# Attention A: one mask matmul goes behind the scores, and TensorE's other work is dealt out anew over the phases

## The chip, the core and the metric

The kernel runs on one core of a Trainium2 chip. The core has five engines that work side by side, each with its own queue of instructions: TensorE (PE in the profile; its weight loads are PEld), VectorE (DVE), ScalarE (ACT), GpSimd (POOL) and SyncE (SP, which here only issues DMAs). TensorE writes to PSUM, eight banks of 128 partitions x 512 F32 values; VectorE and ScalarE read PSUM; GpSimd works on SBUF. The metric is device time in microseconds from the first to the last instruction and what little lies around it; lower is better.

## The reference

The program is a stack of four layers over x of 2 x 1024 x 512 (F32): attention A, a small mixture of experts, attention B, the same mixture again. Each adds its result to x. The change touches attention A alone, cut here to what matters:

```python
q = (query @ Wq).reshape(bsz, tgt_len, 2 * H, D)      # H = 16 heads in pairs, D = 16
k = (query @ Wk).reshape(bsz, tgt_len, 2 * H, D)
v = (query @ Wv).reshape(bsz, tgt_len, H, 2, D)
...                                                    # rotary embedding on q and k
attn1 = causal_attn_pair(q1, k1, v1, v2, mask, scale)  # softmax(q1 k1) v, causal, 1024 x 1024
attn2 = causal_attn_pair(q2, k2, v1, v2, mask, scale)
...
f1 = jnp.fft.rfft(attn1, axis=1)
f2 = jnp.fft.rfft(attn2, axis=1)
attn_freq = f1 - lambda_full * f2                      # then a fixed low-pass filter along time
attn = jnp.fft.irfft(attn_freq * filt, n=tgt_len, axis=1)
...                                                    # RMS norm per head, then @ Wout
```

Query is the layer-normed x. Each of the 16 heads has two score matrices (q1 k1 and q2 k2); since the filter is linear, the kernel subtracts the second softmax, times lambda, from the first before it multiplies by the values, and applies the filter as a small set of matmuls.

## The kernel before, in words

**Units and phases.** Attention A is cut into 16 units (`NU`), each one batch and two heads. A unit has nine phases (`NP`); its rows of 128 queries are j = 0 to 7 for two heads h, and row j needs 128 x (j+1) columns of keys. `PHASES` pairs rows so that each phase has 1024 columns: phases 0 and 1 hold rows 7 of both heads, phases 2 to 7 a row 6, 5 or 4 and a row 0, 1 or 2 of the other head, phase 8 both rows 3. Step t of the main loop issues the scores of phase t (`now`), joins the softmaxes of phase t-1 (`last`) and transposes the weights of phase t-2 (`old`). So "step 7" of a unit is the turn of the loop in which the scores of its phase 7 are issued; it joins phase 6 and transposes phase 5.

**One step on each engine.** The order is written by hand (`tc.manual_schedule`) for TensorE, VectorE, ScalarE and GpSimd; the DMA issues on SP are placed by the framework. The functions named are in the listing below.

- TensorE: `scores` (two mask matmuls per PSUM bank that holds a diagonal block, L475, then the score matmuls, L488; `mm` is 0 for the first score matrix and 1 for the second), four transposes (first half of `transpose`, L578), the step's "large" pieces, four more transposes.
- VectorE: `minima` of the first score matrix (L502 or L510; the scores are held negated, so the least is the softmax's maximum), the reciprocal of `divide` (L545), `minima` of the second, `join` (L554), and what `finish` (L633, L634) has to do.
- ScalarE: the copy of the first four transposes (L580), `exponentials` (L519), the copy of the other four, the copies of the large pieces out of PSUM.
- GpSimd: `share` (L539) and the product in `divide` (L547), which make the factor `ratio` of `join`; then the step's "middle" work, above all `rotate` (three tensor operations, L399 to L401, for half of the time of one unit's q and k); then the "rear" work, above all `fold` (L651 to L654, eight small sums and differences of one unit's result).

**Large pieces.** The tables fill the dictionary `large`, step by step: `project` (four per unit: q and k of the next unit, 256 columns of time each, steps in `PROJECT`), `project_values` (one or two 128-column value tiles, steps in `VALUES`), `weigh` (weights times values; `PARTS` cuts it in two: rows 7, 6, 0 at step 6, the other rows at step 2 of the next unit), `finish` (transposes the sum back and divides it; steps 7, and 4 of the next unit) and, in the first units, `spread_half` (transposes of the second batch's x; `SPREAD`). All pieces of a step share one PSUM bank (`misc`), which comes free when their results have been read. Behind the second and the fourth projection of a unit ScalarE copies the result to `raw`, two DMAs make `other`, and `rotate` runs two steps after the projection (`at(middle, ... + 2, rotate, ...)`), followed by the DMAs to `keys` and, for one half, `swapped`. `fold` of unit n runs in step 6 of unit n+1, behind the step's middle work.

**Scores' buffers.** The score tiles have three buffers of two banks each (`ps_s`); the second score matrix of a phase takes the buffer of the first one of the phase before, so its first matmul waits for that one's exponentials.

Of the kernel before, what the change touches and what calls it, by code (L numbers as in the profile page):

```python
# [2 lines left out]

# [1 line left out]

# [6 lines left out]
F32 = mybir.dt.float32  # L12
# [13 lines left out]
NQ = 4  # L26
# [52 lines left out]
def hybrid_layer_kernel(ctx: ExitStack, tc: tile.TileContext, i: dict, out: bass.AP):  # L79
# [67 lines left out]
    with ExitStack() as sa:  # L147
# [8 lines left out]
        with ExitStack() as sp:  # L156
# [277 lines left out]
            def scores(n, ph):  # L434
                rows = PHASES[ph]
                if ph == 0:
                    least[n] = tally.tile([P, 16, 2], F32, tag="least", name=f"least_{n}")
                    sums[n] = [
                        tally.tile([P, 16], F32, tag=f"sums{mm}", name=f"sums{mm}_{n}") for mm in range(2)
                    ]  # L440
                key = f"{n}_{ph}"
                s = [ps_s.tile([P, T], F32, tag="s", name=f"s{mm}_{key}") for mm in range(2)]
                ps = [
                    work.tile([P, T], F32, tag=f"p{mm}", name=f"p{mm}_{key}", bufs=(4, 2)[mm])
                    for mm in range(2)
                ]
# [24 lines left out]
                opened = {d0 // 512 for d0 in masks}  # L471
                width = P * len(masks) // len(opened)
                for d0 in masks[0 : len(opened)]:
                    for mm in range(2):
                        nc.tensor.matmul(  # L475
                            s[mm][:, d0 : d0 + width],
                            eye[:, 0, :],
                            eye[:, 1 : 1 + width // P, :].rearrange("p k q -> p (k q)"),
                            start=True,
                            stop=False,  # L480
                        )
                ends = {c0 // 512: c0 for _, _, c0, _, _ in pieces}
                for h, j, c0, s0, w in pieces:
                    group, back = (1 - h, T // 2) if s0 >= 512 else (h, 0)
                    q, k = (swapped[n][:, 0, :], swapped[n][:, 1, :]) if s0 >= 512 else (qk[n], keys[n % 2])
                    for mm in range(2):
                        r0 = 64 * group + 32 * mm
                        nc.tensor.matmul(  # L488
                            s[mm][:, c0 : c0 + w],
                            q[r0 : r0 + 32, j * P - back : (j + 1) * P - back],  # L490
                            k[r0 : r0 + 32, s0 - back : s0 - back + w],
                            start=(c0 // 512 not in opened),
                            stop=(ends[c0 // 512] == c0),
                        )
                held[n, ph] = s, ps, spans

            def minima(n, ph, mm):
# [66 lines left out]
            def transpose(n, ph, half):  # L564
# [11 lines left out]
                for k in range(4):  # L576
# [4 lines left out]

            PARTS = [
                (0, 3, [[(0, 7, 0)], [(1, 7, 0)], [(0, 6, 0), (0, 0, P)], [(1, 6, 0), (1, 0, P)]]),
                (
                    3,
                    8,
                    [
                        [(0, 5, 0), (0, 3, P)],  # L590
                        [(1, 5, 0), (1, 3, P)],
                        [(0, 4, 0), (0, 2, P), (0, 1, 2 * P)],
                        [(1, 4, 0), (1, 2, P), (1, 1, 2 * P)],
                    ],
                ),
            ]

            def weigh(bank, c0, n, part):
                _, _, groups = PARTS[part]
                po = bank[:, c0 : c0 + P * (part + 2)]  # L600
# [12 lines left out]
                yield  # L613

                full = P * (part + 1)
                oT = work.tile([P, 3 * P], F32, tag="oT", name=f"oT_{n}_{part}")
                nc.scalar.copy(oT[:, 0:full], po[:, 0:full])
                nc.scalar.copy(oT[64:P, full : full + P], po[64:P, full : full + P])
                turned[n, part] = oT

            def finish(bank, c0, n, part):
                oT = turned[n, part]
                lo, hi, _ = PARTS[part]
# [10 lines left out]
                nc.vector.tensor_mul(  # L634
                    results[n][:, lo:hi, :].rearrange("p r (h f) -> p r h f", h=2),
                    tp.rearrange("p (r h f) -> p r h f", h=2, f=32),
                    rec[:, :, :, None].to_broadcast([P, hi - lo, 2, 32]),
                )
# [47 lines left out]

            SPREAD = [n * NP + k for n in range(6) for k in (1, 5, 8)][1:]
            for j in range(JT):
                t = SPREAD[2 * j]
                at(rear, t - 4, load_x, JT + j)  # L690
# [3 lines left out]
                for half in range(2):  # L694
                    at(large, SPREAD[2 * j + half], spread_half, 256, j, half)
            for half in range(2):
                at(rear, (2 * NQ - 2) * NP + PROJECT[3 - 2 * half], bring, half)
# [776 lines left out]
```

## Time and profile before

| | |
|---|---|
| three runs, median (lowest to highest) | 1141.25 us (1139.06 to 1142.85) |
| the profiled execution, span | 1142.6 us |
| attention A, first to last phase's scores | 35.0 to about 700 us |
| units 10 to 13, first mask to first mask | 40.28 us each |
| units 1 to 6 | 43.24, 41.01, 43.58, 41.00, 41.48, 43.46 us |
| units 7 to 9 | 39.95, 42.05, 41.57 us |
| busy in unit 12: PE, DVE, ACT, POOL | 38.8, 36.5, 36.5, 19.5 us |

The unit lengths are the distances between the first mask matmuls (L475) of consecutive units in the trace. Busy time is a sum over a stretch; it says how much work an engine had, not when it had to wait. In a timeline line, the first number is the start from the span's beginning, the second the duration of the merged instructions, and the bracket gives the idle time of the engine ahead of them and the instruction that ended it. Lines merged as "x4" are four instructions.

### The profile page before, as it was taken

How to read it: one execution, taken by the hardware profiler on the slowest of the kernel's cores; microseconds unless marked ns; L12 is line 12 of the kernel's file. 1: busy time of each engine (PE TensorE's matmuls, PEld its weight loads, DVE VectorE, ACT ScalarE, POOL GpSimd, SP SyncE). 2: the span in 40 equal slices, each digit the busy share in tenths (PEclk: the TensorE clock that was granted, in tenths of full speed). 3: DMA queues.
4: the chain of work that ended last, by engine and by line, in shares of the span. 5: the costliest groups of instructions: out<-in, count | busy, mean ns of one | idle time of the engine just before them, and what ended most of it. 6: DMA issues, size and time to landing. Idle time of an engine off the chain costs nothing.

```text
span 1142.6 us, 23491 instructions
## 1 busy us (share of the span) xinstructions
PE 1067.2 (93%) x8680; PEld 732.3 (64%) x8680; DVE 930.8 (81%) x2046; ACT 766.9 (67%) x2010; POOL 438.1 (38%) x689
## 2 busy tenths in 40 slices
PE   6899999999889999999999979889999999999997
PEld 5777777777677877777777655544555455554554
DVE  5699999999889889889989998577787777758677
ACT  3588988989879889899999877243433433443433
POOL 1246446345345444534535672122323223223300
PEclk9999999999989999999999999889999999999999
DMA  5212222211301101110110521200000000001002
GB/s 176 79 42 67 80 80 66 71 38 52 116 15 39 42 16 38 48 33 25 39 43 16 182 114 39 111 1 1 0 1 1 1 1 1 1 1 37 1 19 92
DMA packets 33345, 52.19 MB, mean 46 GB/s; under 512 B 6480, under 2 KB 11088, under 8 KB 33104
## 3 DMA queue, kind: packets, MB, share of 16 engines
q1 hardware_dynamic: 33072, 50.44, 13.8%
q8 instruction: 69, 1.13, 0.4%
q14 instruction: 44, 0.36, 0.1%
q10 hardware_dynamic: 160, 0.26, 0.1%
HBM read 23.42 MB, written 6.29 MB: 26 GB/s over the span
## 4 chain that ended last, share of the span: by engine, by line
PE 55%; DVE 26%; ACT 11%; issue 5%; POOL 2%; DMA 1%; SPq 0%; DVEq 0%; POOLq 0%; ACTq 0%
DVE least L510 8%; PE s L488 8%; ACT p L519 7%; DVE p L554 6%; PE pq_q L1224 5%; PE py L1287 5%; PE bank L355 4%; PE pq_v L1224 4%; PE dtp L578 4%; PE pq_k L1224 4%; PE z L1028 3%; PE bank L605 3%; DVE least L502 3%; PE hr_f L1092 2%; PE y L978 2%
## 5 line engine op out<-in xcount | busy, mean ns | idle before, releaser
L519 ACT ACTIVATE p<-s,least 128x640 f32<-128x640 f32 (+7 forms) x512 | 378.3, 744 | 41.9 <-DVE least L510 27.9
L510 DVE TENSOR_REDUCE least<-s 128x1 f32<-128x896 f32 (+5 forms) x384 | 244.2, 679 | 35.4 <-PE s L488 35.4
L554 DVE SCALAR_TENSOR_TENSOR p<-p,ratio,p 128x1024 f32<-128x1024 f32 (+7 forms) x256 | 227.0, 922 | 3.5 <-POOL ratio L547 3.4
L578 PE MATMUL dtp<-ident,p 128*128 128x128 f32 x1152 | 184.8, 283 | 14.1 <-ACT dt L580 7.9
L580 ACT COPY dt<-dtp 128x512 f32<-128x512 f32 x288 | 168.9, 586 | 42.9 <-PE dtp L578 39.5
L488 PE MATMUL s<-keys,qk 32*128 32x128 f32 (+3 forms) x1408 | 169.0, 445 | 0.0
L578 PEld LDWEIGHTS dtp<-ident,p 128*128 128x128 f32 x1152 | 128.8, 142 | 58.2 <-ACT dt L580 30.4
L502 DVE TENSOR_REDUCE least<-s 128x1 f32<-128x1024 f32 (+1 forms) x96 | 115.9, 1213 | 26.5 <-PE s L488 26.5
L488 PEld LDWEIGHTS s<-keys,qk 32*128 32x128 f32 x1408 | 94.2, 188 | 49.3 <-issue 43.0
L547 POOL TENSOR_TENSOR ratio<-ratio,inverse 128x2 f32<-128x2 f32 (+1 forms) x144 | 28.1, 195 | 243.0 <-DVE inverse L545 217.9
L539 POOL TENSOR_TENSOR ratio<-sums,neg_lam 128x2 f32<-128x2 f32 (+1 forms) x144 | 73.6, 511 | 117.9 <-ACT p L519 117.6
L355 PE MATMUL bank<-xnT,wqk 128*128 128x256 f32 x472 | 115.8, 389 | 2.8 <-ACT raw L366 1.8
L488 PE MATMUL s<-swapped 32*128 32x128 f32 (+2 forms) x896 | 104.8, 345 | 0.0
L519 ACT ACTIVATION_READ_ACCUMULATOR p<-s,least 128x1 f32 x512 | 104.2, 203 | 0.0
L355 PEld LDWEIGHTS bank<-xnT,wqk 128*128 128x128 f32 x472 | 86.0, 192 | 18.0 <-ACT raw L366 5.6
L488 PEld LDWEIGHTS s<-swapped 32*128 32x128 f32 x896 | 71.0, 185 | 9.5
L475 PE MATMUL s<-eye 128*128 128x256 bf16 (+1 forms) x320 | 60.8, 251 | 16.5 <-ACT p L519 15.5
L605 PE MATMUL bank<-dt,v 128*32 128x128 f32 x2304 | 69.5, 274 | 1.7 <-ACT v L387 0.7
L605 PEld LDWEIGHTS bank<-dt,v 128*32 128x32 f32 x2304 | 60.9, 110 | 8.0 <-ACT v L387 4.4
L400 POOL TENSOR_TENSOR other<-other,rope_a_sb 128x512 f32<-128x512 f32 x30 | 63.0, 2099 | 0.0
L1247 POOL TENSOR_TENSOR qkv_v<-qkv_v,qkv_k 128x512 f32<-128x512 f32 x16 | 20.4, 1274 | 108.5 <-DVE qkv_v L1246 107.4
L379 PE MATMUL bank<-wval,xnT 128*128 128x128 f32 x448 | 60.4, 282 | 0.8
(222 smaller groups left out, 1790.8 us busy)
## 6 DMA issues: line engine op xcount, KB each, us to landing
other<-raw SPq DMA_DIRECT2D x64, 128.0 KB, 2.1
xin<-in_query SPq DMA_DIRECT2D x16, 256.0 KB, 2.9
keys<-qk SPq DMA_DIRECT2D x64, 64.0 KB, 1.9
swapped<-keys SPq DMA_DIRECT2D x32, 128.0 KB, 2.3
x_sb<-in_query SPq DMA_DIRECT2D x16, 256.0 KB, 6.3
out_dram<-x_sb SPq DMA_DIRECT2D x16, 256.0 KB, 2.2
swapped<-qk SPq DMA_DIRECT2D x30, 128.0 KB, 2.3
wqk<-in_w_qk SPq DMA_DIRECT2D x8, 256.0 KB, 2.8
```

The costliest lines, as they stand in the source:

```text
L355: nc.tensor.matmul(pp, wqk[:, part, c, :], xnT[b, half][:, c, t0 : t0 + 256], start=(c == 0), stop=(c == EC - 1),)
L400: engine.tensor_mul(other, other, rope_a[:, 1, cols])
L488: nc.tensor.matmul(s[mm][:, c0 : c0 + w], q[r0 : r0 + 32, j * P - back : (j + 1) * P - back], k[r0 : r0 + 32, s0 - back : s0 - back + w], ...
L502: nc.vector.tensor_reduce(least[n][:, e[0] : e[-1] + 1 : e[-1] - e[0] or 1, mm], s[mm].rearrange("p (g k) -> p g k", g=g), AX.X, ALU.min,)
L510: nc.vector.tensor_reduce(least[n][:, e, mm : mm + 1], s[mm][:, c0 : c0 + w], AX.X, ALU.min)
L519: nc.scalar.activation(ps[mm][:, c0 : c0 + w], sv, AF.Exp, bias=low, scale=-1.0, accum_out=sums[n][mm][:, e : e + 1],)
L539: nc.gpsimd.tensor_mul(ratio[:, w], first, neg_lam.to_broadcast([P, w.stop]))
L554: nc.vector.scalar_tensor_tensor(ps[0][:, c0 : c0 + w], ps[1][:, c0 : c0 + w], ratio[:, k : k + 1], ps[0][:, c0 : c0 + w], ALU.mult, ALU.add,)
L578: nc.tensor.transpose(tp[:, k * P : (k + 1) * P], d[:, c0 : c0 + P], ident)
L580: nc.scalar.copy(dt[:, 4 * half : 4 * half + 4, :], tp.rearrange("p (k q) -> p k q", k=4))
L605: nc.tensor.matmul(po[32 * g : 32 * g + 32, c0 : c0 + P], vals[n // 2 % 2][:, k, 64 * (n % 2) + 32 * h : 64 * (n % 2) + 32 * h + 32], dt[: ...
L1224: nc.tensor.matmul(pq, hTs[n][:, c, :], win(c, s), start=(c == 0), stop=(c == EC - 1))
```

## The change

In `scores`, the mask matmuls of the first score matrix stay ahead; those of the second are issued behind all score matmuls, as the last of their accumulation (the first score matmul of that bank then starts it). `weigh` is cut in three: the second sum (rows 5 to 1) becomes rows 5 and 4 at step 1 of the next unit and rows 3, 2 and 1 at step 2; its transposition (`finish`) goes from step 4 to step 5, except for the last three units. The projections of a unit go from steps 8, 0, 1, 3 to 8, 0, 3, 4, except for the last unit, and the `rotate` of the fourth goes with it from step 5 to step 6. The value tiles are at steps 2, 5, 7 (1, 1, 2 tiles) where they were at 4, 5, 7 (1, 2, 1), with fewer exceptions, and the transposes of the second batch's x at steps 1, 4, 8 where they were at 1, 5, 8; the loads, statistics and scalings of that x are counted from there. `fold` keeps its step 6.

```diff
+                def mask(mm, first):
+                    for d0 in masks[0 : len(opened)]:
                         nc.tensor.matmul(
                             s[mm][:, d0 : d0 + width],
                             eye[:, 0, :],
                             eye[:, 1 : 1 + width // P, :].rearrange("p k q -> p (k q)"),
-                            start=True,
-                            stop=False,
+                            start=first,
+                            stop=not first,
                         )
-                ends = {c0 // 512: c0 for _, _, c0, _, _ in pieces}
+                mask(0, True)
...
                 for h, j, c0, s0, w in pieces:
...
+                        if bank not in opened:
+                            start = True
+                        else:
+                            start = mm == 1 and begins[bank] == c0
...
+                            start=start,
+                            stop=ends[bank] == c0 and not (mm == 1 and bank in opened),
                         )
+                mask(1, False)
...
-            PARTS = [
-                (0, 3, [[(0, 7, 0)], [(1, 7, 0)], [(0, 6, 0), (0, 0, P)], [(1, 6, 0), (1, 0, P)]]),
...
+            PARTS = [(0, 3), (3, 8)]
+            WEIGHED = [
+                (0, 0, True, [[(0, 7, 0)], [(1, 7, 0)], [(0, 6, 0), (0, 0, P)], [(1, 6, 0), (1, 0, P)]]),
+                (1, 0, False, [[(0, 5, 0)], [(1, 5, 0)], [(0, 4, 0)], [(1, 4, 0)]]),
+                (1, P, True, [[(0, 3, 0)], [(1, 3, 0)], [(0, 2, 0), (0, 1, P)], [(1, 2, 0), (1, 1, P)]]),
             ]
...
-                for blocks in zip(*order):
-                    for g, (h, j, c0, k) in enumerate(blocks):
+                for blocks in zip_longest(*order):
+                    for g, block in enumerate(blocks):
+                        if block is None:
+                            continue
+                        h, j, c0, k = block
...
-                oT = work.tile([P, 3 * P], F32, tag="oT", name=f"oT_{n}_{part}")
-                nc.scalar.copy(oT[:, 0:full], po[:, 0:full])
-                nc.scalar.copy(oT[64:P, full : full + P], po[64:P, full : full + P])
-                turned[n, part] = oT
+                if base == 0:
+                    turned[n, part] = work.tile(
+                        [P, (part + 2) * P], F32, tag=f"oT{part}", name=f"oT_{n}_{part}", bufs=1
+                    )
+                oT = turned[n, part]
+                nc.scalar.copy(oT[:, base : base + P], po[:, 0:P])
+                if half:
+                    nc.scalar.copy(oT[64:P, base + P : base + 2 * P], po[64:P, P : 2 * P])
...
-                for part, (t_sum, t_end) in enumerate(((6, 7), (NP + 2, NP + 4 - (n >= NU - 2)))):
-                    at(large, t + t_sum, weigh, P * (part + 2), n, part)
-                    at(large, t + t_end, finish, (192, 320)[part], n, part)
+                for piece, when in enumerate((6, NP + 1, NP + 2)):
+                    at(large, t + when, weigh, (2, 1, 2)[piece] * P, n, piece)
+                for part, when in enumerate((7, NP + (5 if n < NU - 3 else 4 if n < NU - 2 else 3))):
+                    at(large, t + when, finish, (192, 320)[part], n, part)
                 at(rear, t + NP + (3 if n == NU - 1 else 6), fold, n)
...
-            PROJECT = (-1, 0, 1, 3)
-            VALUES = {p: [(k, w) for k, w in ((-14, 1), (-13, 2), (-11, 1), (-5, 1), (-4, 2), (-2, 1))] for p in range(1, 8)}
-            VALUES[4] = [(-5, 1), (-4, 2), (-2, 1), (0, 1), (4, 1), (5, 2)]
-            VALUES[5] = [(-11, 1), (-10, 1), (-9, 1), (-8, 1), (-5, 1), (-4, 2), (-2, 1)]
-
-            SPREAD = [n * NP + k for n in range(6) for k in (1, 5, 8)][1:]
+            PROJECT = [(-1, 0, 3, 4)] * (NU - 1) + [(-1, 0, 1, 3)]
+            VALUES = {p: [(-16, 1), (-13, 1), (-11, 2), (-7, 1), (-4, 1), (-2, 2)] for p in range(1, 8)}
+            VALUES[4] = [(-13, 1), (-11, 2), (-7, 1), (-7, 1), (-4, 1), (-2, 2)]
+
+            SPREAD = [n * NP + k for n in range(6) for k in (1, 4, 8)][1:]
...
-                    if t + PROJECT[piece] >= 0:
-                        at(large, t + PROJECT[piece], project, 256, u, piece)
+                    when = t + PROJECT[u][piece]
+                    if when >= 0:
+                        at(large, when, project, 256, u, piece)
                     if piece % 2:
-                        at(middle, t + PROJECT[piece] + 2, rotate, u, 1 - piece // 2)
+                        at(middle, when + 2, rotate, u, 1 - piece // 2)
```

More of the change, by code (lines that the diff above doesn't have):

```diff
@@ L2 @@
 from contextlib import ExitStack
+from itertools import zip_longest
 import numpy as np
@@ L472, in scores @@
                 width = P * len(masks) // len(opened)
-                for d0 in masks[0 : len(opened)]:
-                    for mm in range(2):
+                def mask(mm, first):
+                    for d0 in masks[0 : len(opened)]:
                         nc.tensor.matmul(
@@ L478, in scores @@
                             eye[:, 1 : 1 + width // P, :].rearrange("p k q -> p (k q)"),
-                            start=True,
-                            stop=False,
-                        )
-                ends = {c0 // 512: c0 for _, _, c0, _, _ in pieces}
+                            start=first,
+                            stop=not first,
+                        )
+                mask(0, True)
+                begins, ends = {}, {}
+                for _, _, c0, _, _ in pieces:
+                    begins.setdefault(c0 // 512, c0)
+                    ends[c0 // 512] = c0
                 for h, j, c0, s0, w in pieces:
@@ L485, in scores @@
                     q, k = (swapped[n][:, 0, :], swapped[n][:, 1, :]) if s0 >= 512 else (qk[n], keys[n % 2])
+                    bank = c0 // 512
                     for mm in range(2):
                         r0 = 64 * group + 32 * mm
+                        if bank not in opened:
+                            start = True
+                        else:
+                            start = mm == 1 and begins[bank] == c0
                         nc.tensor.matmul(
@@ L491, in scores @@
                             k[r0 : r0 + 32, s0 - back : s0 - back + w],
-                            start=(c0 // 512 not in opened),
-                            stop=(ends[c0 // 512] == c0),
+                            start=start,
+                            stop=ends[bank] == c0 and not (mm == 1 and bank in opened),
                         )
+                mask(1, False)
                 held[n, ph] = s, ps, spans
@@ L580, in transpose, with weigh @@
                 nc.scalar.copy(dt[:, 4 * half : 4 * half + 4, :], tp.rearrange("p (k q) -> p k q", k=4))
-            PARTS = [
-                (0, 3, [[(0, 7, 0)], [(1, 7, 0)], [(0, 6, 0), (0, 0, P)], [(1, 6, 0), (1, 0, P)]]),
[L586 to L595, printed above, removed]
-            ]
-            def weigh(bank, c0, n, part):
-                _, _, groups = PARTS[part]
-                po = bank[:, c0 : c0 + P * (part + 2)]
+            PARTS = [(0, 3), (3, 8)]
[3 more added lines that the diff above has]
+                (1, P, True, [[(0, 3, 0)], [(1, 3, 0)], [(0, 2, 0), (0, 1, P)], [(1, 2, 0), (1, 1, P)]]),
+            ]
+            def weigh(bank, c0, n, piece):
+                part, base, half, groups = WEIGHED[piece]
+                po = bank[:, c0 : c0 + P * (1 + half)]
                 order = [[(h, j, c0, k) for h, j, c0 in g for k in range(j + 1)] for g in groups]
-                for blocks in zip(*order):
-                    for g, (h, j, c0, k) in enumerate(blocks):
+                for blocks in zip_longest(*order):
[3 more added lines that the diff above has]
+                        h, j, c0, k = block
                         dt, at = turned[n, h, j, k]
@@ L613, in weigh @@
                 yield
-                full = P * (part + 1)
-                oT = work.tile([P, 3 * P], F32, tag="oT", name=f"oT_{n}_{part}")
-                nc.scalar.copy(oT[:, 0:full], po[:, 0:full])
-                nc.scalar.copy(oT[64:P, full : full + P], po[64:P, full : full + P])
-                turned[n, part] = oT
+                if base == 0:
[6 more added lines that the diff above has]
+                    nc.scalar.copy(oT[64:P, base + P : base + 2 * P], po[64:P, P : 2 * P])
             def finish(bank, c0, n, part):
                 oT = turned[n, part]
-                lo, hi, _ = PARTS[part]
+                lo, hi = PARTS[part]
                 tp = bank[:, c0 : c0 + 64 * (hi - lo)]
@@ L696, in hybrid_layer_kernel @@
             for half in range(2):
-                at(rear, (2 * NQ - 2) * NP + PROJECT[3 - 2 * half], bring, half)
+                at(rear, (2 * NQ - 2) * NP + PROJECT[2 * NQ - 1][3 - 2 * half], bring, half)
             for k in range(4):
```

## The prediction

> **What bounds the kernel now.** I read the page first.
>
> ```profile
> span 1142.6 us, 23491 instructions
> PE 1067.2 (93%) x8680; PEld 732.3 (64%) x8680; DVE 930.8 (81%) x2046; ACT 766.9 (67%) x2010; POOL 438.1 (38%) x689
> PE 55%; DVE 26%; ACT 11%; issue 5%; POOL 2%; DMA 1%; SPq 0%; DVEq 0%; POOLq 0%; ACTq 0%
> ```
>
> TensorE leads, VectorE stands next, POOL has more than half of its time free. Busy sums by unit of nine phases say the same of attention A (units 11 and 12):
>
> ```profile
> core 0: us, PE busy (x) PEld busy (x) DVE busy (x) ACT busy (x) POOL busy (x), PEclk, DMA share, GB/s
> 492.90:533.20 40.30, 38.93 (x452) 30.94 (x450) 36.60 (x60) 36.60 (x94) 19.49 (x32) 1.00 0.12 34
> 533.20:573.40 40.20, 38.84 (x451) 30.86 (x449) 36.51 (x60) 36.52 (x94) 19.49 (x32) 1.00 0.12 35
> ```
>
> So TensorE idles 1.4 us a unit: all that a better deal could win. But averages hide order. POOL's timeline of unit 12, phases 5 to 7 (start, duration):
>
> ```profile
> 558.49 0.20 POOL L547 TENSOR_TENSOR ratio<-ratio,inverse 128x2 f32<-128x2 f32 x1 [2.34 <-DVE inverse L545]
> 558.64 1.28 POOL L399 TENSOR_TENSOR raw<-raw,rope_a_sb 128x512 f32<-128x512 f32 x1
> 559.88 1.98 POOL L400 TENSOR_TENSOR other<-other,rope_a_sb 128x512 f32<-128x512 f32 x1
> 561.94 1.35 POOL L401 TENSOR_TENSOR qk<-raw,other 128x512 f32<-128x512 f32 x1
> 563.24 0.19 POOL L539 TENSOR_TENSOR ratio<-sums,neg_lam 128x2 f32<-128x2 f32 x1
> 563.56 0.20 POOL L547 TENSOR_TENSOR ratio<-ratio,inverse 128x2 f32<-128x2 f32 x1
> 563.71 0.46 POOL L651 TENSOR_TENSOR folded<-result 128x128 f32<-128x128 f32 x1
> ...
> 567.33 0.46 POOL L654 TENSOR_TENSOR folded<-result 128x128 f32<-128x128 f32 x1
> 567.74 0.20 POOL L539 TENSOR_TENSOR ratio<-sums,neg_lam 128x2 f32<-128x2 f32 x1
> 568.01 0.20 POOL L547 TENSOR_TENSOR ratio<-ratio,inverse 128x2 f32<-128x2 f32 x1
> ```
>
> POOL is a queue in program order. `rotate` (L399 to L401) fills the time between the ratios of steps 5 and 6, `fold` (L651 to L654) that between steps 6 and 7, with no gap in either. VectorE's `join` (L554) needs the ratio (L547):
>
> ```profile
> 559.45 2.69 DVE L554 SCALAR_TENSOR_TENSOR p<-p,ratio,p 128x768 f32<-128x768 f32 x2
> 564.52 1.46 DVE L554 SCALAR_TENSOR_TENSOR p<-p,ratio,p 128x768 f32<-128x768 f32 x2
> 568.82 1.41 DVE L554 SCALAR_TENSOR_TENSOR p<-p,ratio,p 128x640 f32<-128x640 f32 x2
> 570.43 0.36 DVE L634 TENSOR_TENSOR result<-bank,rec 128x192 f32<-128x192 f32 x1
> ```
>
> Step 7's ratio is ready at 568.21, its join starts at 568.82: 0.6 us of slack. What a late ratio does is seen once, in unit 6, where `rotate` waited 2.9 us for a DMA (DVE's, then PE's timeline, then sums by stretch):
>
> ```profile
> 318.31 1.78 DVE L554 SCALAR_TENSOR_TENSOR p<-p,ratio,p 128x768 f32<-128x768 f32 x2 [2.09 <-POOL ratio L547]
> 319.64 0.63 PE L578 MATMUL dtp<-ident,p 128*128 128x128 f32 x4 [1.63 <-DVE p L554]
> 318.00:320.00 2.00, 0.37 (x6) 0.39 (x4) 1.69 (x2) 0.69 (x4) 1.84 (x5) 1.00 0.18 66
> 322.00:324.00 2.00, 1.35 (x13) 0.99 (x15) 1.79 (x4) 2.00 (x8) 1.48 (x4) 0.50 0.00 0
> ```
>
> VectorE stood 2.09, TensorE 1.63 us, the granted clock fell to 0.5, and the unit took 43.5 us against 40.3.
>
> **TensorE's pieces, from piece to piece in unit 12.** Projection 1.73; value tile 0.99, two 1.89; old second sum 2.32 (80 instructions, ten rounds of 8); `finish` 0.57 and 0.46. The split sum needs six and five rounds: 1.39 and 1.16, so 0.23 more. Old to new: phase 1, 1.73 to 1.39; phase 2, 2.32 to 1.16+0.99=2.15; phase 4, 0.57+0.99=1.56 to 1.73; phase 5, 1.89 to 0.57+0.99=1.56; phase 7, 0.46+0.99=1.45 to 0.46+1.89=2.35; the others stay. Phases 0 to 5 lose 0.67, phase 7 gains 0.90. ACT's extra copy (0.29, phase 1) replaces one of 0.39 and hides in the ACT time that is free in each unit (3.8 us); the two `oT` tags only take waits away.
>
> **The mask.** Same matmuls and weight loads. VectorE may start one mask (about 0.11 us) sooner, and the wait for the second bank (15.5 us in 25 waits, "PE s L475 <- ACT p L519") comes one mask and one matmul pair later, some 0.3 us (phase 1's two masks and twelve score instructions take 1.29, 0.1 each). Bounds: nothing, and 25 x 0.3 = 7.5 us won; extra changes between BF16 and F32 show no gap at today's one per phase, so I allow at most 144 x 0.05 = 7 us lost. I take 2 us won, as most of these waits lie in a few units.
>
> **The step that decides.** The fourth projection moves from phase 3 to 4, and `rotate` follows two phases behind: into phase 6, where `fold` is. On POOL then stand, behind step 6's ratio: `rotate`, `fold`, and only then both instructions of step 7's ratio. Behind that ratio on VectorE: join 7, the reciprocal and product of `finish`, which frees the one bank that phase 8's projection is written to, and minima 8; on TensorE the transposes of step 8. The rotation's DMAs on SP (two for `keys`; `swapped` belongs to the other half, still in phase 2) come one phase later: about X+10 us against scores at X+16, X being the start of step 6's scores; hidden.
>
> **Smaller moves, costed at nothing.** The other half's `rotate` stays in phase 2; step 3's ratio follows it with 0.6 us to spare before its join (550.0 against 550.65), and the phase shrinks by 0.17. Three of eight `norm_scale` (POOL, 2.08 us) go from phase 4 to 3, behind that ratio; the next ratio is wanted over 4 us later. Their loads of x on SP go one phase earlier with their statistics, the distance stays. `bring` of the first half follows the projection from step 57 to 58, as does the rotation that waits for it. Pair 1's value weights are issued at the end of step 0 and now wanted in step 2 (about 5 us later; a 256 KB load lands in 2.8 us, and one of x goes ahead): 0 to 1 us lost once, taken as nothing. Pair 4's value tiles move to units 6 and 7; their x was brought in steps 54 and 58, the first tile that needs the later half comes in step 65.
>
> Round trip of a unit, old and new, in us:
> - Projection 8 to next scores (571.16 to 573.43): 2.27, 2.27.
> - Scores 0 to scores 6: 26.59; 26.59-0.67=25.92.
> - Scores 6 (559.76) to the end of step 6's ratio (563.76): 4.00. In step 5 VectorE's join falls from 2.69 to about 1.5 (step 6's, without L400 beside it, takes 1.46) and `finish` adds 0.67, so it comes to minima 6 earlier by some 0.5 against its own queue, 0.34 against TensorE's scores: I take 3.66. The stretched join is now step 6's; it ends at X+7.4 and lies inside the wait that follows.
> - That end to the end of step 7's ratio: old 4.45 (568.21). New: rotate 4.65+0.08, fold, ratio 0.47. Fold took 4.08 beside a join; with its two stretched instructions at their 0.32 it is 3.3. VectorE then has no join left, so I take 3.3: 8.5 (9.3 with 4.08).
> - Ratio to projection 8: old 2.95 (not what bounds). New: join and `finish` 1.97 (568.82 to 570.79), handing over 0.35 to 0.4: 2.35.
> Sums: 40.26 and 42.7. A steady unit grows by 2.4 us.
>
> Units 1 to 13 have the collision (unit 0 has no fold; unit 15's projections stay, so unit 14 has none). By unit lengths, from the first mask matmul of each:
> - 10 to 13: 40.28 each, +2.4: 9.6.
> - 7 to 9: 123.57 together, as pair 4's values crowd there; new 3 x 42.7 + 0.99 = 129.1: 5.5.
> - 6: 43.46; its DMA wait of 2.9 stays, now ahead of both: 45.6: 2.1.
> - 5: 41.48; two spreads of 0.33: 43.4: 1.9.
> - 2 and 4: 41.0; three spreads: 43.7: 5.4.
> - 1 and 3: 43.24 and 43.58; VectorE's 1.0 of statistics in phase 5 as well: 44.7: 2.6.
> Together 27.1. Tail: the first half of the last sum leaves the drain, -1. Mask: -2.
>
> **The clock.** Between scores 8 and projection 8 TensorE now idles 2.4 + 0.6 us around 0.55 of transposes. In unit 6 idle stretches of 1.63, 0.36 and 0.65 brought 6.83 us at 0.5. Bounds: nothing, and 3.4 us lost in each unit. I take one spell of 3.41 us (the shortest in the record) in eight units of ten, 1.5 us lost: 1.2 x 12 = 14.4. [...]
>
> Sum: 1142.6+27.1+14.4-3 = 1181.1; the profiled execution is 1.35 above the median of three runs, so 1180.
>
> **Rivals.**
> - *Faster.* The fold doesn't hold up step 7's ratio. It decides where ratio to ratio stays under 4.45+0.6+1.0 (slack, and what earlier steps gain), some 6.0 us: rotate and ratio alone (5.2) fit. Then the even deal shows: TensorE's waits in phases 4 to 7 (0.10, 0.07, 0.32, 0.31 in unit 12) go, 0.8 us in 13 units: 1141.25-10.4 = 1131. For: joins lose their worst overlap, TensorE's fullest phase shrinks. Against: at 567.74 exactly this ratio starts as the fold ends, and at 563.24 the one before it as `rotate` ends.
> - *Full clock.* The stall is as above, but the clock holds: 1165. For: 1.31 us idle at 678 brought no fall.
> - *Clock falls for two spells each time, and fold takes 4.08*: with 2.5 us lost to the clock, 1142.6+27.1+13x0.8+13x2.5-3-1.35 = 1208.
> - *The stall is half caught up* from VectorE's 3.7 free us a unit (40.3-36.6), the clock and the mask cancelling: 1141.25+27.1/2 = 1155. Against: TensorE, not VectorE, sets the pace after it.
>
> **How the numbers follow.** Collision with clock loss 50%, with full clock 22%, two spells 9%, half caught up 8%, faster 8%, no change (the fold's delay and the gains cancel) 3%. 0.3% (3.4 us) is what a measurement can tell from none. Range 1153 to 1204: it leaves out the faster and unchanged cases and most of the two-spell one, some 18%. Faster 0.08, same 0.03, slower 0.89.
>
> **What would show it.** Right: POOL L651 directly behind L401, L539 behind L654; "DVE p L554 <- POOL ratio L547" from 3.4 us to 30 or more; "PE dtp L578 <- DVE p L554" from 2.2 to 20 or more; units near 43 to 45; spells at 0.5. Wrong: units at or under 40.3 with no such wait, which would mean that the fold runs elsewhere; or waits as said with no fall of the clock.

## The result and the profile after

The changed kernel takes 1182.11 us (median of 4 runs, 1179.66 to 1184.63) where the kernel before takes 1140.44 us: 1.0355 times as long, 95% interval [1.0325, 1.0385]. 1180 us was forecast.

The page of the changed kernel, lines as shown of before. Its line numbers are moved: the mask is L477, the scores L500, `minima` L515 and L523, `join` L567, the ratio L552 and L560, `rotate` L400 to L402, `fold` L663 to L666, the transposes L591, the projection L356.

```profile
span 1177.2 us, 23508 instructions
PE 1091.6 (93%) x8680; PEld 743.2 (63%) x8680; DVE 933.2 (79%) x2046; ACT 768.6 (65%) x2025; POOL 430.0 (37%) x689
PE 56%; DVE 18%; ACT 12%; POOL 9%; issue 4%; DMA 1%; POOLq 0%; SPq 0%; DVEq 0%; ACTq 0%
```

The engines' work has hardly changed. PE's busy time grew by 24 us with the same number of matmuls: 13 of them are the slower clock below (number 2, which has the same matmuls and far less time at that clock, is busy for 1078.6 us), the other 11 come without it. But GpSimd's share of the chain that ended last went from 2% to 9%. GpSimd was never the busiest engine; it is now the one waited for. Its timeline in unit 13, steps 6 and 7 (start, duration):

```profile
636.70 0.20 POOL L560 TENSOR_TENSOR ratio<-ratio,inverse 128x2 f32<-128x2 f32 x1 [2.48 <-DVE inverse L558]
636.85 1.28 POOL L400 TENSOR_TENSOR raw<-raw,rope_a_sb 128x512 f32<-128x512 f32 x1
638.09 1.98 POOL L401 TENSOR_TENSOR other<-other,rope_a_sb 128x512 f32<-128x512 f32 x1
640.15 1.33 POOL L402 TENSOR_TENSOR qk<-raw,other 128x512 f32<-128x512 f32 x1
641.44 0.45 POOL L663 TENSOR_TENSOR folded<-result 128x128 f32<-128x128 f32 x1
...
644.28 0.45 POOL L666 TENSOR_TENSOR folded<-result 128x128 f32<-128x128 f32 x1
644.69 0.19 POOL L552 TENSOR_TENSOR ratio<-sums,neg_lam 128x2 f32<-128x2 f32 x1
644.96 0.20 POOL L560 TENSOR_TENSOR ratio<-ratio,inverse 128x2 f32<-128x2 f32 x1
```

Between the two ratios stand `rotate` (4.6 us) and `fold` (3.3 us), one behind the other. The same stretch on VectorE, then on TensorE, where each bracket gives the idle time and what ended it:

```profile
645.19 1.41 DVE L567 SCALAR_TENSOR_TENSOR p<-p,ratio,p 128x640 f32<-128x640 f32 x2 [2.38 <-POOL ratio L560]
...
646.81 0.36 DVE L646 TENSOR_TENSOR result<-bank,rec 128x192 f32<-128x192 f32 x1
```

```profile
646.22 0.63 PE L591 MATMUL dtp<-ident,p 128*128 128x128 f32 x4 [1.57 <-DVE p L567]
647.62 1.99 PE L356 MATMUL bank<-xnT,wqk 128*128 128x256 f32 x8 [0.78 <-ACT v L388]
```

The same two pieces of TensorE's work before, in unit 12, without a wait:

```profile
570.53 0.66 PE L578 MATMUL dtp<-ident,p 128*128 128x128 f32 x4
571.16 1.99 PE L355 MATMUL bank<-xnT,wqk 128*128 128x256 f32 x8
```

GpSimd releases VectorE, VectorE releases TensorE, and TensorE waits a second time for its PSUM bank. The bank is handed over by a ScalarE copy (L388, the value tiles of that step), which itself stood waiting for VectorE's product L646 (it ends at 647.17):

```profile
647.20 0.37 ACT L388 COPY v<-bank 128x256 f32<-128x256 f32 x1 [2.33 <-DVE result L646]
```

It ends at 647.57, and the projection starts at 647.62. So the late ratio reaches TensorE twice, once through the join and once through `finish` and this copy. From first mask to first mask, steps 0 to 7 together became shorter by 0.2 to 0.5 us in units 10 to 13, and step 8 went from 4.41 us there to 6.8 (7.4 in unit 1) where the clock held, and to 8.3 to 9.9 in the other units. Over units 1 to 13, step 8 gained 42 us (105.1 against 62.7), and all other steps lost 6.

The units with the longer step 8 are those in which the granted clock fell. Busy sums of the changed kernel by stretches of 2 us at the end of unit 11 (the column after the engines is the granted clock):

```profile
558.00:560.00 2.00, 0.77 (x5) 0.56 (x6) 1.90 (x5) 0.57 (x2) 0.00 (x0) 1.00 0.00 0
560.00:562.00 2.00, 2.00 (x6) 1.57 (x7) 2.00 (x4) 1.73 (x6) 0.20 (x1) 0.53 0.00 0
```

The trace has eight spells (unbroken stretches) at 0.5 in units 1 to 13: six of 3.41 us and two of 6.83. The projection behind the stall takes 3.56 us in unit 11 instead of the 1.99 of unit 13, and 3.12 to 3.62 us in the eight units.

### The profile page after: what moved, and what is told of

It reads as the page before. It is cut to its first block, busy times and chain, and to the rows that moved or that the text cites. A ratio compares the mean times of both kernels' runs of the same rounds, so it can differ in the third digit from the quotient of the medians.

```text
span 1177.2 us, 23508 instructions
## 1 busy us (share of the span) xinstructions
PE 1091.6 (93%) x8680; PEld 743.2 (63%) x8680; DVE 933.2 (79%) x2046; ACT 768.6 (65%) x2025; POOL 430.0 (37%) x689
## 4 chain that ended last, share of the span: by engine, by line
PE 56%; DVE 18%; ACT 12%; POOL 9%; issue 4%; DMA 1%; POOLq 0%; SPq 0%; DVEq 0%; ACTq 0%
PE bank L356 7%; ACT p L532 7%; PE s L500 6%; DVE least L523 5%; PE dtp L591 5%; PE py L1300 4%; PE pq_q L1237 4%; PE pq_v L1237 4%; PE pq_k L1237 4%; DVE p L567 4%; PE z L1041 3%; PE hr_f L1105 2%; PE y L991 2%; PE bank L614 2%; POOL other L401 2%
## 5 line engine op out<-in xcount | busy, mean ns | idle before, releaser
L523 DVE TENSOR_REDUCE least<-s 128x1 f32<-128x896 f32 (+5 forms) x384 | 244.0, 678 | 35.7 <-PE s L500 35.5
L567 DVE SCALAR_TENSOR_TENSOR p<-p,ratio,p 128x1024 f32<-128x1024 f32 (+7 forms) x256 | 228.3, 927 | 31.2 <-POOL ratio L560 31.2
L591 PE MATMUL dtp<-ident,p 128*128 128x128 f32 x1152 | 182.9, 282 | 28.9 <-DVE p L567 21.6
L500 PE MATMUL s<-keys,qk 32*128 32x128 f32 (+3 forms) x1408 | 178.8, 440 | 1.6 <-ACT p L532 1.5
L591 PEld LDWEIGHTS dtp<-ident,p 128*128 128x128 f32 x1152 | 134.6, 144 | 54.3 <-issue 27.8
L515 DVE TENSOR_REDUCE least<-s 128x1 f32<-128x1024 f32 (+1 forms) x96 | 115.8, 1213 | 32.4 <-PE s L500 32.1
L356 PE MATMUL bank<-xnT,wqk 128*128 128x256 f32 x472 | 128.1, 419 | 10.2 <-ACT v L388 8.2
L560 POOL TENSOR_TENSOR ratio<-ratio,inverse 128x2 f32<-128x2 f32 (+1 forms) x144 | 28.1, 195 | 288.0 <-DVE inverse L558 263.7
L500 PEld LDWEIGHTS s<-keys,qk 32*128 32x128 f32 x1408 | 98.3, 186 | 38.1 <-issue 26.8
L552 POOL TENSOR_TENSOR ratio<-sums,neg_lam 128x2 f32<-128x2 f32 (+1 forms) x144 | 74.2, 515 | 120.2 <-ACT p L532 119.9
L356 PEld LDWEIGHTS bank<-xnT,wqk 128*128 128x128 f32 x472 | 92.0, 205 | 31.4 <-ACT v L388 13.4
L500 PE MATMUL s<-swapped 32*128 32x128 f32 (+2 forms) x896 | 105.9, 348 | 0.0
L614 PE MATMUL bank<-dt,v 128*32 128x128 f32 x2304 | 76.1, 275 | 2.3 <-ACT oT L629 0.8
L500 PEld LDWEIGHTS s<-swapped 32*128 32x128 f32 x896 | 71.3, 187 | 10.2 <-issue 0.3
L477 PE MATMUL s<-eye 128*128 128x256 bf16 (+1 forms) x320 | 77.1, 258 | 0.0
L401 POOL TENSOR_TENSOR other<-other,rope_a_sb 128x512 f32<-128x512 f32 x30 | 63.6, 2120 | 0.0
```

The lines of the kernel that those rows point to most:

```text
L356: nc.tensor.matmul(pp, wqk[:, part, c, :], xnT[b, half][:, c, t0 : t0 + 256], start=(c == 0), stop=(c == EC - 1),)
L401: engine.tensor_mul(other, other, rope_a[:, 1, cols])
L477: nc.tensor.matmul(s[mm][:, d0 : d0 + width], eye[:, 0, :], eye[:, 1 : 1 + width // P, :].rearrange("p k q -> p (k q)"), start=first, stop ...
L500: nc.tensor.matmul(s[mm][:, c0 : c0 + w], q[r0 : r0 + 32, j * P - back : (j + 1) * P - back], k[r0 : r0 + 32, s0 - back : s0 - back + w], ...
L515: nc.vector.tensor_reduce(least[n][:, e[0] : e[-1] + 1 : e[-1] - e[0] or 1, mm], s[mm].rearrange("p (g k) -> p g k", g=g), AX.X, ALU.min,)
L523: nc.vector.tensor_reduce(least[n][:, e, mm : mm + 1], s[mm][:, c0 : c0 + w], AX.X, ALU.min)
```

## The experiments

The theory: GpSimd's queue, in program order, holds step 7's ratio behind `rotate` and `fold`, and the stall costs a second time through the clock. The rivals: TensorE's new deal itself (2.35 us of pieces in step 7, the split sum), the mask's new place, a late rotation as such. In the diffs, `...` stands for lines left out. All ratios are to runs of the kernel before on the same chip.

**1. The rotation back to step 5, all else as changed.**

```diff
-                        at(middle, when + 2, rotate, u, 1 - piece // 2)
+                        at(middle, when + (1 if piece == 3 and u < NU - 1 else 2), rotate, u, 1 - piece // 2)
```

> The changed kernel, with the rotation of a unit's later half put back to step 5 (one step behind its projection instead of two); fold stays in step 6, every TensorE piece stays where the change put it. Theory (GpSimd's queue: rotate and fold one behind the other hold up step 7's ratio): the stall in phase 8 goes (8.3 to 4.3 us in the units with a clock spell, 6.8 to 4.3 in the others), VectorE's wait for the ratio falls from 31.2 us to under 5, the spells at half clock between 160 and 605 us go; time about 1134 (1127 to 1142). Rival (TensorE's new deal itself costs the time: 2.35 us of pieces in phase 7, the split sum, the mask behind the scores): still 1175 or more.

Measured: 1150.88 us, 1.0075 [1.0051, 1.0098]. Most of the loss is gone, so the deal is not what cost the most, but 17 us more are left than the theory said. Waits of this kernel (in total, times, longest), and its GpSimd in unit 12:

```profile
POOL raw L400 <- DMA other<-raw: 25.6, 11, 5.5
DVE p L567 <- POOL ratio L560: 16.6, 21, 4.5
```

```profile
564.15 1.39 POOL L400 TENSOR_TENSOR raw<-raw,rope_a_sb 128x512 f32<-128x512 f32 x1 [1.51 <-DMA other<-raw]
```

With one step between a projection and its rotation, the DMAs that build `other` have not landed, and GpSimd stands waiting for them with the ratios behind it. The expectation left that out. This kernel swaps one delay in GpSimd's queue for a smaller one; it doesn't tell the theory from the rivals cleanly. The next one does.

**2. Fold moved out of the way, the rotation left in step 6.** The unit's result is kept in two tiles, the smaller one twice, so that the next unit may write.

```diff
-                    results[n] = work.tile([P, JT, 64], F32, tag="result", name=f"result_{n}", bufs=1)
+                results[n, part] = work.tile(
+                    [P, hi - lo, 64], F32, tag=f"result{part}", name=f"result_{n}_{part}", bufs=2 - part
+                )
...
-                at(rear, t + NP + (3 if n == NU - 1 else 6), fold, n)
+                at(rear, t + NP + (3 if n == NU - 1 else 6 if n >= NU - 3 else 8), fold, n)
```

> The changed kernel, with fold of units 0 to 12 moved from step 6 to step 8 of the next unit (its result in two tiles, the smaller one twice, so that the next unit may write); rotate stays in step 6. Theory (it is the two being one behind the other ahead of step 7's ratio, not rotate's place): the stall goes as well, about 1134 (1127 to 1142), perhaps lower than with rotate in step 5 since VectorE's fullest step (5) is free of the rotation. Rival 1 (rotate in step 6 alone is too late, for the keys or for the joins): 1160 or more. Rival 2 (TensorE's deal): 1175 or more.

Measured: 1137.47 us, 0.9950 [0.9933, 0.9968]. The stall is gone, with every TensorE piece and the rotation where the change put them; steady units take 40.0 us. GpSimd in unit 12:

```profile
559.27 1.33 POOL L402 TENSOR_TENSOR qk<-raw,other 128x512 f32<-128x512 f32 x1
560.56 0.19 POOL L552 TENSOR_TENSOR ratio<-sums,neg_lam 128x2 f32<-128x2 f32 x1
560.89 0.19 POOL L560 TENSOR_TENSOR ratio<-ratio,inverse 128x2 f32<-128x2 f32 x1
...
565.17 0.19 POOL L560 TENSOR_TENSOR ratio<-ratio,inverse 128x2 f32<-128x2 f32 x1 [2.39 <-DVE inverse L558]
565.32 0.46 POOL L668 TENSOR_TENSOR folded<-result,result 128x128 f32<-128x128 f32 x1
```

Step 7's ratio now directly follows the rotation, GpSimd then idles for 2.39 us ahead of step 8's, and the fold begins behind that. VectorE waits 2.2 us for ratios in all, where it waits 31.2 us in the changed kernel, and units 1 to 13 hold no spell at 0.5 (the mean granted clock of the profile is 0.988, in the changed kernel's 0.977).

**3. The mask alone, on the kernel before.** `scores` as in the change, nothing else.

```diff
-                for d0 in masks[0 : len(opened)]:
-                    for mm in range(2):
+                def mask(mm, first):
+                    for d0 in masks[0 : len(opened)]:
...
+                mask(0, True)
...
+                mask(1, False)
```

> The kernel before with only the second mask behind the scores. Theory: 0 to 5 us won, 1136 to 1141, and the wait of 'PE s L475 <- ACT p L519' (15.5 us in 25 waits) nearly gone. Rival (the mask is what costs: switching between BF16 and F32 once more per phase, or the second bank ready later): 1150 or more.

Measured: 1135.28 us, 0.9936 [0.9914, 0.9958], and once more, beside another kernel below:

> The mask alone on the kernel before, once more and beside the combined version, since the comparison of both needs less than one per cent: 1135 (1133.5 to 1136.5), 0.6% under the kernel before. Rival (its gain was between chips): within 0.3% of the kernel before.

Measured: 1134.26 us, 0.9937 [0.9913, 0.9961], on another chip. The mask is a gain of 0.6%, some 7 us, a little more than was expected; steady units take 39.69 us against 40.28. The wait of the mask for ScalarE's exponentials, 15.5 us before, is gone; 0.3 us of it are left, now in front of the scores.

**4. The late rotation alone, on the kernel before.**

```diff
-                        at(middle, t + PROJECT[piece] + 2, rotate, u, 1 - piece // 2)
+                        at(middle, t + PROJECT[piece] + (3 if piece == 3 and u < NU - 1 else 2), rotate, u, 1 - piece // 2)
```

> The kernel before with only the later half's rotation one step later, in step 6, ahead of fold; its projection stays in phase 3. Theory (GpSimd's queue): 2 to 2.5 us in each of 13 units and 8 to 10 spells at half clock: 1172 (1162 to 1185). Rival (the new deal is needed for the loss): within 5 us of 1140.

Measured: 1189.44 us, 1.0408 [1.0377, 1.0439]. One step's shift of one piece of GpSimd work, 14 times in the kernel, costs 47 us with nothing of the new deal in place. Two waits of this kernel stand where they stand in the changed one (31.2 and 21.6 us there, 3.4 and 2.2 before):

```profile
DVE p L554 <- POOL ratio L547: 30.4, 16, 2.4
PE dtp L578 <- DVE p L554: 22.8, 14, 1.7
```

It is more than was expected, and more than the whole change: units 1 to 13 hold eleven spells of the lower clock, three of them of 6.83 us (mean granted clock 0.971).

**5. The stall's idle time filled.** The changed kernel, with ten matmuls of no use ahead of step 8's first transposes.

```diff
+FILL = 10
...
                 tp = turning(f"dtp_{n}_{ph}_{half}")
+                if half == 0 and ph == 6 and 0 < n < NU - 2:
+                    for _ in range(FILL):
+                        nc.tensor.matmul(
+                            tp[:, 0 : 2 * P],
+                            eye[:, 0, :],
+                            eye[:, 1:3, :].rearrange("p k q -> p (k q)"),
...
```

> The changed kernel, with ten extra BF16 matmuls (identity times mask, into the bank that the next transposes overwrite) ahead of the first transposes of step 8 in units 1 to 13, where TensorE stood idle for 1.57 us; they compute nothing that is used. Theory (a stall costs twice, once as waiting and once as a spell at half clock): the spells between 160 and 605 us go, the wait stays; all 13 units take what those without a spell take, about 42.3 us; 1182 - 15 = 1167 (1162 to 1172). Rival (the spells only fill time that would be waited for anyway): within 4 us of 1182, or slower by the extra work.

Measured: 1167.29 us, 1.0222 [1.0204, 1.0240]. TensorE in unit 11 and that unit's sums:

```profile
547.96 1.25 PE L592 MATMUL dtp<-eye 128*128 128x256 bf16 x10
549.61 0.66 PE L601 MATMUL dtp<-ident,p 128*128 128x128 f32 x4 [0.39 <-DVE p L568]
```

```profile
510.90:553.40 42.50, 40.59 (x462) 31.82 (x459) 36.62 (x60) 36.71 (x95) 18.84 (x33) 1.00 0.11 33
```

The first transposes still start when the join releases them (the wait shrank to 0.39 us, since the filling stands in it), VectorE waits as long for the ratio as before (31.3 us), and no spell at half clock is left in units 1 to 13 (1.00 granted in units 11 and 12, 0.991 in the mean of the profile): all steady units take 42.5 us. Useless work made the kernel 15 us faster. With number 2, which has no stall but the same deal and mask, the 3.55% split up: 2.72% (31 us) is the wait (1.0222 against 0.9950), 1.33% (15 us, 10 to 21 by the ends of both intervals) the clock (1.0355 against 1.0222), and 0.5% (6 us) is what mask, deal and the later fold win together.

**6. The changed kernel with both masks ahead again.** `scores` as before, all else as changed.

```diff
-                def mask(mm, first):
-                    for d0 in masks[0 : len(opened)]:
+                for d0 in masks[0 : len(opened)]:
+                    for mm in range(2):
...
-                mask(0, True)
...
-                mask(1, False)
```

> The changed kernel with both masks ahead of the scores again. From the mask alone on the kernel before (7 us won): 1182 + 7 = 1189 if its gain adds to the deal. Rival (the gain is swallowed by the stall, which GpSimd's queue paces): within 3 us of 1182.

Measured: 1182.72 us, 1.0372 [1.0329, 1.0416], against 1.0355 with the mask moved. The mask's gain doesn't show. In the profiles a unit without a spell takes 42.75 us here (unit 13) and 42.33 us there, so 5 us may be left of it; the two intervals are too wide to tell that from nothing, and the spells differ too (eight of 3.41 us in units 1 to 13 here, 27 us together, against 34 us there).

**7. Rotation late, fold later, mask moved, TensorE dealt out as before.** On the kernel of number 3, the result in two tiles as in number 2.

```diff
-                        at(middle, t + PROJECT[piece] + 2, rotate, u, 1 - piece // 2)
+                        at(middle, t + PROJECT[piece] + (3 if piece == 3 and u < NU - 1 else 2), rotate, u, 1 - piece // 2)
...
-                at(rear, t + NP + (3 if n == NU - 1 else 6), fold, n)
+                at(rear, t + NP + (3 if n == NU - 1 else 6 if n >= NU - 3 else 8), fold, n)
```

> The kernel before with the second mask behind the scores, the later half's rotation in step 6 and fold of units 0 to 12 in step 8: the late rotation that alone cost 47 us, with the fold out of its way. Theory (only the two together block): no stall, 1133 (1129 to 1137), a little under the mask alone (1135) as VectorE's fullest step loses the rotation. Rival (a late rotation is harmful by itself): 1150 or more.

Measured: 1132.92 us, 0.9916 [0.9894, 0.9939]. The late rotation that costs 47 us in front of the fold costs nothing once the fold is behind step 8's ratio. Against number 2, which differs by the deal alone, this is 0.34% less: the new deal, by itself, wins nothing and loses perhaps 4 us (the intervals just touch). Steady units take 39.82 us here and 40.0 there, four of units 1 to 5 and unit 7 are 0.3 to 1.0 us longer with the new deal, while units 8 and 9 are shorter with it.

**8. The split sum alone**, both pieces in step 2, on the kernel of number 3; `weigh` is as in the change.

```diff
-                for part, (t_sum, t_end) in enumerate(((6, 7), (NP + 2, NP + 4 - (n >= NU - 2)))):
-                    at(large, t + t_sum, weigh, P * (part + 2), n, part)
...
+                for piece, when in enumerate((6, NP + 2, NP + 2)):
+                    at(large, t + when, weigh, (2, 1, 2)[piece] * P, n, piece)
...
```

> The kernel before with the second mask behind the scores and the second sum in two pieces, both in step 2 (eleven rounds where there were ten, one copy more on ScalarE); all else at its old step. Theory: 0.23 us a unit more than the mask alone: 1135 + 3.5 = 1138.5 (1135 to 1142). Rival (the split costs nothing since VectorE paces): 1135.

Measured: 1134.59 us, 0.9934 [0.9914, 0.9954], steady units 39.70 us: the eleventh round costs nothing that can be seen.

**9. A combination.** Number 7 without the two exceptions in `VALUES`, so that all pairs' value tiles lie at the same steps.

```diff
-            VALUES[4] = [(-5, 1), (-4, 2), (-2, 1), (0, 1), (4, 1), (5, 2)]
-            VALUES[5] = [(-11, 1), (-10, 1), (-9, 1), (-8, 1), (-5, 1), (-4, 2), (-2, 1)]
```

> The kernel before with the second mask behind the scores, the later half's rotation in step 6, fold in step 8, and every pair's value tiles at the same steps (the two exceptions for pairs 4 and 5 left out). Units 8 and 9 then lose what they carried beyond the others (41.6 and 41.2 against 39.8 us): 3.2 us won, half a microsecond given back in unit 6: 1132.9 - 2.7 = 1130 (1127 to 1133). Rival (unit 6 has no room for pair 4's tiles, or x of the second batch lands too late for them): 1133 or more.

Measured: 1130.14 us (6 runs, 1129.86 to 1130.80), 0.9902 [0.9882, 0.9922]: 1% under the kernel before and 4.4% under the changed one. Units 6 to 13 all take 39.8 us, units 8 and 9 took 41.6 and 41.2 in number 7; the two intervals overlap, so it is these lengths that show the step from number 7 to this one.

## Why the prediction was right, step by step

*The step that decides* was read right: the rotation moved in front of the fold, and step 7's ratio behind both. Numbers 2, 4 and 7 show it from both sides: take the fold away and the loss is gone, move the rotation alone and the loss is there, and move both and it is gone again. That GpSimd's queue runs in program order, and that step 7's ratio had 0.6 us of slack, could be read in the timeline before.

*The round trip.* Forecast and measured in unit 13, which has no spell: projection 8 to scores 2.27 and 2.27; scores 0 to scores 6 25.92 and 25.78; scores 6 to the end of the ratio 3.66 and 3.56 (633.34 to 636.90); ratio to ratio 8.5 and 8.26 (to 645.16), with the fold at its unhindered 3.29; ratio to projection 8 2.35 and 2.46 (to 647.62). Together 42.7 and 42.3. What frees the bank for that projection is not `finish` itself, as the prediction has it, but the ScalarE copy behind it; it was in the 0.35 to 0.4 us that the prediction gave to handing over, and it now copies two value tiles (0.37 us) where it copied one (0.29).

*By units.* 27.1 us was the sum without the clock. The filled kernel, where no clock falls, gives 24.5 us in its profile for units 1 to 13 (562.9 against 538.4). One term was wrong: "6: its DMA wait of 2.9 stays, now ahead of both: 45.6". It took 41.7 us, without a wait for that DMA. In the trace the rotation now comes due 5.4 us after its DMAs were issued (327.79, 333.15); before, it came due 3.3 us after (307.84, 311.10), and they took 6.15 us to land. They are also issued 2.6 us behind the load of x that goes ahead of them (L342), not 0.7; which of the two saves the wait no run separates. With the rotation in step 5 this unit also scatters (42.9 and 40.9 us in two profiles of number 3). The profile before holds that wait, and the changed kernel's profile is of its fastest run, which is part of why the two profiled spans differ by 34.6 us and the medians by 41.7. In the filled kernel the other units of 1 to 13, with units 7 to 9 taken together, were within 0.7 us of the forecast, units 1 to 5 each 0.3 to 0.6 us above it. That the total came within 2 us is in part luck: these errors cancel some of that of unit 6.

*The moves costed at nothing* were not quite that: unit 0 takes 40.7 us in number 2 against 38.8 with the mask alone, of which a spell of 3.41 us in its step 2 is one part; the rest was not taken apart.

*The clock.* Forecast 14.4 us, measured 15 (12 by the lengths of units 1 to 13 in the two profiles): eight units of thirteen were hit where eight of ten were forecast, but two of them with a spell of twice the length; that the two errors cancel is luck. In the changed kernel a stall is a first gap of 1.55 to 1.75 us and, behind transposes of 0.63 us (1.09 in unit 2), a second of 0.78 us (1.22 in units 1 and 3, 0.32 in unit 2); eight of thirteen brought the fall. In the filled kernel 0.39 and 0.84 us behind 1.25 us of filling (unit 11) brought none, there or in the other twelve.

Where the stalls that were hit lie can be read from the trace of the changed kernel. The eight spells of units 1 to 13 begin at 160.76, 208.55, 256.33, 300.71, 430.41, 515.75, 560.12 and 604.49 us, that is 14, 14, 13, 38, 25, 13 and 13 times 3.413 us apart. These are the stretch of that length ahead of the spell at the end of unit 11, and the two, 25 and 26 such lengths later, that share the stall of unit 13, where the clock held:

```profile
556.71:560.12 3.41, 1.05 (x7) 0.68 (x6) 2.59 (x5) 1.07 (x4) 0.75 (x4) 1.00 0.00 0
642.04:645.45 3.41, 2.60 (x31) 2.03 (x29) 1.03 (x3) 2.83 (x9) 2.94 (x10) 1.00 0.11 38
645.45:648.86 3.41, 1.87 (x10) 1.53 (x11) 3.31 (x7) 1.39 (x3) 0.20 (x1) 1.00 0.00 0
```

TensorE is busy for 0.31 of the first and for 0.76 and 0.55 of the other two: both gaps of unit 11 lie in one stretch, those of unit 13 in two. With all of units 1 to 13 of the changed kernel cut in this way, the stretches ahead of the eight spells are busy for 0.56 (unit 2) and for 0.31 to 0.42 (the seven others), and the emptiest one of each of the five stalls that were not hit for 0.52 to 0.55. Ahead of the spell in unit 6 of the kernel before, 3.413 us are busy for 0.48. The 0.56 of unit 2 lies above all five that were not hit, and no run set this share on purpose: what decides between a fall and none was not shown.

*The mask.* "I take 2 us won" was mis-sized, though inside its bounds: alone the mask wins 7. The step that failed is that its 25 waits for a second bank were priced as the main part. In a steady unit that wait was 0.3 us, in step 7; it is gone, and step 7 is as long as it was (4.75 us); in number 3 TensorE's sum of step 6 (`weigh`) stands in the chain of what ended last there. The unit shrank by 0.59 all the same, in steps 0, 2, 5 and 8 for the most part. The chain before ran through VectorE from step 4 to step 8, and where it does, minima that start 0.1 us sooner can pass on whole; that would fit steps 5 and 8, it leaves 0 and 2 open, and no run shows it by itself. In the changed kernel, where GpSimd sets the pace of step 8, it is not to be told from nothing (number 6).

*The extra round of the sum*, costed at 0.23 us a unit, costs nothing (number 8), though it is TensorE's; *the new deal* was expected to gain 0.67 us in steps 0 to 5. They take 25.78 us in unit 12 of number 2 against 26.59 before, but 26.10 with the mask alone: 0.32 is the deal's. Steps 6 to 8 give it back even without the collision (14.24 us in number 2, 13.59 in number 3).

*The rivals.* Full clock (1165) is the filled kernel, 1167; that it would be the case was wrong. Faster (1131) is what number 2 was to be: it comes out at 1137, so even with the ratio in time the deal wins less than the 0.8 us a unit that the rival allowed. Half caught up (1155) is ruled out by the filled kernel, whose units are 24.5 of the forecast 27.1 us longer at full clock. Two spells each time (1208) came in two units of thirteen.

## What to carry to other kernels

When work is moved on an engine that is half idle, write down its queue between the two instructions that others wait for, not its busy time: here 8 us stood in a gap of 4.5. A piece that has slack of its own should stand behind the next thing that is waited for, not ahead of it, and the cure that worked here was to move the piece that nobody waits for. If a stall can't be removed, look at the granted clock behind it, since part of its price may be the clock's: here 15 us of 46, the other 31 being the wait.

## What the runs showed of the hardware that was not expected

- Stalls with 2.1 to 2.8 us of idle time in 3.0 to 3.4 us, 13 of them, brought the granted clock to 0.5 in eight places (the changed kernel), and with ten small BF16 matmuls in each (1.25 us, number 5) it fell in none; they made the kernel 15 us faster though their results are thrown away. The length of the first gap does not tell the hit places (1.55 to 1.75 us) from the others (1.56 to 1.57).
- All spells at 0.5 between 35 and 700 us last 3.41 or 6.83 us: one of each in the kernel before, six and three in the changed one.
- With one or two BF16 mask matmuls less in front of F32 scores, and as many behind, the additional changes between the two types cost nothing that can be seen: in steps 6 and 7 of unit 13 of the changed kernel scores, mask and transposes follow one another without idle time in the timeline (633.34 to 635.54 and 638.02 to 640.03 us), and the mask alone makes the kernel 7 us faster (number 3).
- VectorE's join and GpSimd's rotation lengthen each other where they meet: the join takes 2.7 us beside the rotation, in step 5 before and in step 6 after, against 1.4 to 1.5 without it, and the rotation's second operation (L400 before, L401 after) takes 1.98 us beside the join, but 1.28 where VectorE was waiting (unit 6 before).
